# In-degree sums started in the encoder, and the general edge path moved to the program's end with a second copy of the network

## The chip, the core and the metric

The kernel runs on one core of a Trainium2 chip. A core has five engines, each with an instruction queue of its own that is worked off in order: PE (matrix multiplication; its weight loads are listed as PEld), DVE (vector), ACT (scalar), POOL (general purpose) and SP (which here only starts transfers). Sixteen DMA engines move data between the chip's memory and the core's on-chip memory. Engines wait for one another by semaphores. The metric is the device time of one execution in microseconds (us).

## The reference

The inputs are 1,250 nodes with 1,024 features and 20,000 edges (`src`, `dst`), sorted by `dst`. Two graph networks run one after the other, each inside a residual and a normalisation:

```python
h = layernorm(x, ln_in_g, ln_in_b)
h = relu(h @ W1 + b1) @ W2 + b2                      # encoder, 1024 -> 512 -> 256
for i in range(3):                                   # three layers
    agg = segment_sum(h[src], dst, num_segments=n)
    z = relu((h + agg) @ layer_Wa[i] + layer_ba[i]) @ layer_Wb[i] + layer_bb[i]
    h = h + relu(layernorm(z, layer_ng[i], layer_nb[i]))
delta = relu(h @ Wd1 + bd1) @ Wd2 + bd2              # decoder
x1 = norm(x + layernorm(x + delta, out_g, out_b))
...
deg = segment_sum(ones, dst); deg_inv = 1 / max(deg, 1)
h1  = relu(x1 @ W_self0 + (segment_sum(x1[src], dst) * deg_inv) @ W_neigh0 + b0)
out = h1 @ W_self1 + (segment_sum(h1[src], dst) * deg_inv) @ W_neigh1 + b1
out = norm(x1 + out)
```

The second network needs `deg`, the number of edges that end at each node: its in-degree.

## The kernel before, in words

**Nodes and numbers.** The nodes stand in ten tiles of 128 (the last one has 98 nodes and four spare rows). An fp32 matmul is made from three: each operand is split into a high and a low part (`split_w`, `relu_split`; ACT makes the high part, DVE or POOL the low one, L124, L125, L150 to L155), and `mm3` (L113 to L115) adds high x high, high x low and low x high. Names ending in h and l are these parts.

**Edges as a matrix.** All sums over edges are done with one dense matrix `A` of 1,254 x 1,254 edge counts (ten tiles of rows, AW columns). It is built during the encoder. The sorted edges stand in 157 tiles of 128, five to a group. For each group DVE builds one-hot matrices `R` (L333) and `Q` (L342, L344) from two arrays of codes (`rp`, `qp`) which `codes(0)` to `codes(2)` compute; PE multiplies them (`edge_tile`, L358) into `pa`, and ACT copies the block to `A` at a column that it reads from `anci` (`load_bases` L321, copy L364). POOL adds the one column that two groups share (L370). `ahead` and `some_edges` put these steps between the matmuls of the encoder.

**A fast and a general path.** This needs that each group's edges lie in a window of at most 51 nodes. The array `est` carries the edges, the windows' starts `anc` and their limits `atop`, `agap`. At the start DVE counts how many limits hold; the flag `fli` is 1 when some do not (L270, L272). `anci` is `anc` limited from above by `atop` (L264). `nc.values_load(fli)` (L389) loads the flag into a register on all five engines. `any_edges`, called before the encoder's second chunk of nodes, branches on it (L392): if it is set, `general_adjacency` builds the matrix from any edges, in the tile `acc` and scratch tiles (`spare` among them), and writes it to memory; a second branch (L578) loads it over `A`. With these inputs the flag is 0 and both branches are passed by.

**The encoder** goes over five chunks `PCH` of two tiles each. For a chunk: transposes of x (`transpose_x`, L445; ACT and DVE split the result into `h0h`, `h0l`, L448, L450), four column blocks `y_chunk(c, f)` of x @ W1 (with edge matmuls between them), and `h_rows(t)`, the product with W2, for each of the two tiles. `SLOTS` = 13 of these blocks carry edges. After the last of them the identity is added to `A` (L577), since h + agg is (A + 1) h.

**The layers.** `agg(i, c, t0, t1)` multiplies h by `A` for a range of columns (L649); ACT and DVE split the sum into `zh` and `zl` (L654, L655); `z1_chunk` and `z2_rows` are the layer's two products. Weights come through a ring of three buffers, `wraw`; `load_wab`, `load_Wd1` and `load_Wd2` (L615, L698, L707) fetch and split them. `load_xo` has SP write the output bias as rows of `xo_d` (L732) and POOL add x to them in memory by accumulating transfers (L736). `A` is written to `A_d` (L781) in layer 0, after the loads of the next layer's vectors. The second network reads it back.

**In-degrees.** `asum` is the sum of A's ten row tiles; `degrees()` (L601 to L606, in layer 1) sums it over the partitions, subtracts the identity and inverts. Before, tiles 0 to 5 are added ahead of layer 0 in five instructions of 1,254 columns (L744, L746), and tiles 6 to 9 in eight halves of 627 columns that the source has in layer 0 (L784).

**What sets the order.** In `manual_schedule` stretches (the start, the encoder's first chunk, and everything from the decoder's main loop on) the listed engines follow the source. Elsewhere a scheduler lays out each engine's queue by its own estimates; so an instruction can come earlier or later than its place in the source, but no instruction crosses a branch.

Of the kernel before, what the change touches and what calls it, by code (L numbers as in the profile page):

```python
# [21 lines left out]
P = 128  # L22
# [33 lines left out]
def gz(t):  # L56
    return P if t < NT - 1 else N - (NT - 1) * P + NG
# [3 lines left out]
    return P if t < NT - 1 else N - (NT - 1) * P  # L61


@with_exitstack
def tile_gnn(ctx, tc, x, es, vecs, W1, W2, b2, Wa, Wb, bb, ng, nb, Wd1, Wd2, bd2, og, ob,
             Ws0, Wn0, b0l, Ws1, Wn1, b1l, out):
    nc = tc.nc
    V, S, G, T = nc.vector, nc.scalar, nc.gpsimd, nc.tensor

# [95 lines left out]
    S1 = tc.alloc_tile_pool(name="S1", bufs=1, reuse_waits="tile")  # L165
    epsc0 = S1.tile([P, 1], F32, name="epsc0")

    est = S1.tile([P, 2 * NGR * GT + 3 * (NGR + 1) + 3 * GT], I32, name="est")
    ne, o = NGR * GT, 2 * NGR * GT
    esrc, edst = est[:, :ne], est[:, ne:o].rearrange("p (g j) -> p g j", j=GT)  # L170
    anc, atop, agap = (est[:, o + i * (NGR + 1):o + (i + 1) * (NGR + 1)] for i in range(3))
    o += 3 * (NGR + 1)
    woff, wwid, wend = (est[:, o + i * GT:o + (i + 1) * GT].unsqueeze(1).broadcast_to([P, NGR, GT])
                        for i in range(3))
    base, nbase = (anc[:, i:i + NGR].unsqueeze(2).broadcast_to([P, NGR, GT]) for i in range(2))
# [56 lines left out]
    with tc.high_priority(), tc.manual_schedule(engines=order):  # L232
        V.memset(epsc, EPS)
        S.activation(epsc0, epsc, AF.Sqrt)
        V.memset(ones, 1.0)
        iq = S1.tile([P, NT * WMAX], F16, name="iq")
        G.iota(iq, pattern=[[1, NT * WMAX]], base=1, channel_multiplier=0, allow_small_or_imprecise_dtypes=True)
        ir = S1.tile([P, P], BF16, name="ir")
        G.iota(ir, pattern=[[1, P]], base=0, channel_multiplier=0, allow_small_or_imprecise_dtypes=True)
        make_identity(nc, ident)  # L240
        dd, dn, blk = (S1.tile([P, NGR, GT], I32, name=nm_) for nm_ in ("dd", "dn", "blk"))
        va, vn = (S1.tile([P, NGR, GT], F32, name=nm_) for nm_ in ("va", "vn"))

        rp = S1.tile([P, NGR * GT, 2], BF16, name="rp")
        qp = S1.tile([P, NGR * GT, 2], F16, name="qp")
        q4 = S1.tile([P, NGR], F32, name="q4")
        vcnt = S1.tile([P, 1], F32, name="vcnt")
        anci = S1.tile([1, NGR + 1], I32, name="anci")
        ac, ad = (S1.tile([1, NGR + 1], F32, name=nm_) for nm_ in ("ac", "ad"))
        acnt = S1.tile([1, 2], F32, name="acnt")  # L250
        V.tensor_sub(dd, edst, base)
        V.tensor_sub(dn, edst, nbase)
        V.tensor_sub(dd, dd, woff)

        V.tensor_sub(ad[:, :NGR], anc[0:1, 1:], anc[0:1, :NGR])
        V.tensor_tensor(vn, dn, wend, ALU.is_lt)
        V.tensor_tensor(va, dd, wwid, ALU.is_lt)
        V.scalar_tensor_tensor(ac, anc[0:1], 0.0, atop[0:1], ALU.add, ALU.is_le, accum_out=acnt[:, 0:1])
        V.scalar_tensor_tensor(va, dd, 0.0, va, ALU.is_ge, ALU.mult)
        V.scalar_tensor_tensor(ad[:, :NGR], ad[:, :NGR], 0.0, agap[0:1, :NGR], ALU.add, ALU.is_le,  # L260
                               accum_out=acnt[:, 1:2])
        V.scalar_tensor_tensor(va, vn, 1.0, va, ALU.mult, ALU.mult, accum_out=vcnt)
        V.scalar_tensor_tensor(vcnt[0:1], acnt[:, 0:1], acnt[:, 1:2], vcnt[0:1], ALU.add, ALU.add)
        V.tensor_tensor(anci, anc[0:1], atop[0:1], ALU.min)  # L264
        warm_up(WA)
        st0 = bn(0)
        pc = pst("pc")
        T.matmul(pc[:1, 0:1], vcnt, ones[:, 0:1], start=True, stop=True)
        flf = S1.tile([1, 1], F32, name="flf")
        V.tensor_scalar(flf, pc[:1, 0:1], E + 2 * NGR + 0.5, None, ALU.is_lt)  # L270
        fli = S1.tile([1, 1], I32, name="fli")
        V.tensor_copy(fli, flf)  # L272
        warm_up(WB)

    def pairs(ap):
# [97 lines left out]

    def ahead(g):
        nonlocal n_oh
        while n_oh < min(NGR, g):
            one_hots(n_oh)
            n_oh += 1

    def some_edges(k):  # L380
        nonlocal n_ed
        for _ in range(k):
            ahead(n_ed // GT + LOOK + 1)
            if n_ed < ET:
                edge_tile(n_ed)
                n_ed += 1


    flag = nc.values_load(fli[0:1, 0:1], min_val=0, max_val=1)  # L389
    def any_edges():  # L390

        with tc.If(flag > 0):  # L392
            acc = Ap.tile([P, NT, AW], F32, name="acc", tag="A")
            V.memset(acc, 0.0)
            scratch = [B1.tile([P, 8 * (PW + 2)], F32, name=f"g{s}", tag=f"h0{s}0", bufs=1) for s in "hl"] + spare
            general_adjacency(tc, psp, acc[:, :, :N], (esrc, est[:, ne:2 * ne]), ident, ones, x, A_g, xg_d, scratch)
            res = Ap.tile([P, NT, AW], F32R, name="A", tag="A")
            nc.sync.dma_start(res.bitcast(F32)[:, :, :NN], A_g)
        return res


# [100 lines left out]
    with tc.manual_schedule(engines=order):  # L502
# [17 lines left out]
        warm_up(WC)  # L520
        transpose_x(0, (2,))
        split_W1(2)
        mv2 = bn_mv(bn(2), 2)
        split_W1(3)
        std2 = bn_std(mv2)
        split_W1(4)
        next(bn_norm(2, *std2))
        codes(0)
        for f in range(4):
            first[f] = pst("ps_y", "ps" if f < 2 else "pa")  # L530
        for k in range(8):
# [4 lines left out]
            if k == 0:  # L536
                transpose_x(0, (4,))
                split_W1(5)
                codes(1)
                mv3 = bn_mv(bn(3), 3)  # L540
            if k == 2:
                transpose_x(0, (6,))
# [1 line left out]
                std3 = bn_std(mv3)  # L544
                split_W1(7)
                next(bn_norm(3, *std3))
                codes(2)
            if k == 6:
                transpose_x(1, (0,))
        transpose_x(1, (2,))  # L550
        transpose_x(1, (4, 6))
        load_W2()
        V.tensor_copy(onesr, ones)
        ahead(2)
    for f in range(4):
        V.tensor_add(b1c[:, f:f + 1], first[f][:, PW:PW + 1], vec[:, C_B1 + f:C_B1 + f + 1])
    NC = len(PCH)
    SLOTS = 13
    for c in range(NC):
        if c == 1:  # L560
            A = any_edges()
        for f in range(4):
            slot = 4 * (c - 1) + f
            y_chunk(c, f, -(-(ET - n_ed) // (SLOTS - slot)) if 0 <= slot < SLOTS else 0)
# [5 lines left out]
            if f in (1, 2):  # L570
                if 2 * c + 3 + f < NT:
                    ln_x(2 * c + 3 + f)
            if slot == SLOTS - 1:

                for t in range(NT):
                    n = gz(t)
                    V.tensor_add(A[:n, t, t * P:t * P + n], A[:n, t, t * P:t * P + n].bitcast(F32), ident[:n, :n])  # L577
                with tc.If(flag > 0):  # L578
                    nc.sync.dma_start(A.bitcast(F32)[:, :, :NN], A_g)
    for t in PCH[NC - 1]:  # L580
        h_rows(t)
    B1.release()
# [158 lines left out]
    load_wab(0)  # L741
    begin_layer(0)
    load_xo()
    V.tensor_add(asum, A[:, 0, :NN].bitcast(F32), A[:, 1, :NN].bitcast(F32))  # L744
    for t in range(2, 6):
        V.tensor_add(asum[:gz(t)], asum[:gz(t)], A[:gz(t), t, :NN].bitcast(F32))  # L746
    for t0, t1 in ((0, 8), (8, NT)):
        agg(0, 0, t0, t1)
        agg(0, 1, t0, t1)
    for i in range(3):  # L750
# [28 lines left out]
        if i == 0:  # L779
            with tc.issue_after(loads["nb"].ins):  # L780
                nc.sync.dma_start(A_d, A.bitcast(F32)[:, :, :NN])  # L781
            for t in range(6, NT):
                for cs in (slice(0, NN // 2), slice(NN // 2, NN)):
                    V.tensor_add(asum[:gz(t), cs], asum[:gz(t), cs], A[:gz(t), t, cs].bitcast(F32))  # L784
            load_wab(2)
            for k in range(2):
                load_Wd2(k)
# [881 lines left out]
```

## Time and profile before

| | us |
|---|---|
| median of 3 timed runs | 923.88 (922.95 to 924.91) |
| the profiled execution | 923.78 |
| its span, first to last instruction | 921.9 |
| stage: encoder, to the last encoder rows | 0 to about 122 |
| stage: three layers | about 122 to 255 |
| stage: decoder | about 255 to 360 |
| stage: second network | about 360 to 919 |
| last ACT instruction (L1268) | 917.89, 0.81 long |
| issue of the last two output transfers (SP, L1269) | 918.34, 0.81 for both |

The page's second part shows the span in 40 equal slices of 23 us:

```profile
PE   7799998999899999999999999999999999999997
DVE  8799678595976775565677675547466786777785
...
PEclk9799999999999999999999999999999999999999
DMA  7310058953115649997442236537895722322214
```

Each digit is the busy share of a slice in tenths, PEclk the clock that PE was granted in tenths of full speed. The rows of instructions that follow below give start, duration and engine, and in brackets how long the engine had been idle and what ended that. "PEq", "DVEq" and so on are an engine's instruction sequencer, which handles branches and register loads.

### The profile page before, as it was taken

What the parts mean: (1) busy time and instruction counts of PE and PEld (TensorE: products, weight loads), DVE (VectorE), ACT (ScalarE), POOL (GpSimd) and SP (SyncE); (2) the same over time, 40 slices, a digit from 0 to 9 for tenths busy, and PEclk for the clock granted to TensorE, in tenths of its full rate; (3) what the DMA queues carried; (4) which work ended last, traced back from release to release, by engine and by line L of the source; (5) the groups of instructions that cost most, each with busy time, mean ns of one, the idle gap of its engine ahead of it and who ended that gap; (6) DMA issues with size and microseconds to landing.
All of it is one profiled execution on the core that took longest, in us unless ns stands there. A gap on an engine that the chain in (4) does not pass through costs nothing.

```text
span 921.9 us, 13248 instructions
## 1 busy us (share of the span) xinstructions
PE 894.7 (97%) x4777; PEld 788.2 (85%) x4783; DVE 645.0 (70%) x1311; ACT 394.2 (43%) x760; POOL 87.7 (10%) x122
## 2 busy tenths in 40 slices
PE   7799998999899999999999999999999999999997
PEld 6799998988887778999988888889999888888885
DVE  8799678595976775565677675547466786777785
ACT  4577523454566873211133354543111333333454
POOL 4022234344201000000000000000000000000000
PEclk9799999999999999999999999999999999999999
DMA  7310058953115649997442236537895722322214
GB/s 243 118 42 2 1 197 217 312 177 103 61 52 202 224 145 348 336 310 254 170 148 72 77 127 197 172 125 264 287 306 214 235 80 77 85 72 76 81 47 177
DMA packets 83666, 148.35 MB, mean 161 GB/s; under 512 B 8296, under 2 KB 31995, under 8 KB 83082
## 3 DMA queue, kind: packets, MB, share of 16 engines
q1 hardware_dynamic: 77206, 126.90, 41.4%
q0 software_dynamic: 2176, 10.27, 4.5%
q10 hardware_dynamic: 4212, 10.27, 3.0%
q8 instruction: 38, 0.62, 0.3%
q14 instruction: 34, 0.28, 0.1%
HBM read 103.35 MB, written 49.21 MB: 165 GB/s over the span
## 4 chain that ended last, share of the span: by engine, by line
PE 83%; DVE 6%; DMA 4%; ACT 1%; issue 1%; POOL 0%; ACTq 0%; DVEq 0%; POOLq 0%; SPq 0%
PE ps_A L1222 20%; PE ps_m L113 14%; PE ps_m L115 14%; PE ps_m L114 14%; DMA wraw<-in_Wd_dram 3%; PE ps_dd L113 2%; PE ps_dd L115 2%; PE ps_dd L114 2%; PE pa L358 2%; PE ps_y L113 2%; PE ps_y L114 1%; PE ps_y L115 1%; PE ps_z L649 1%; DVE asum L746 1%; PE pt L974 1%
## 5 line engine op out<-in xcount | busy, mean ns | idle before, releaser
L113 PE MATMUL ps_m<-w,th 128*128 128x512 f32 x520 | 204.1, 392 | 0.0
L115 PE MATMUL ps_m<-w,th 128*128 128x512 f32 x520 | 202.6, 390 | 0.0
L114 PE MATMUL ps_m<-w,th 128*128 128x512 f32 x520 | 202.3, 389 | 0.0
L1222 PE MATMUL ps_A<-A,qh 128*128 128x418 f32 (+1 forms) x480 | 170.5, 355 | 0.0
L1222 PE MATMUL ps_A<-A,ql 128*128 128x418 f32 (+1 forms) x480 | 169.9, 354 | 0.0
L115 PEld LDWEIGHTS ps_m<-w,th 128*128 128x128 f32 x520 | 97.6, 188 | 20.7
L113 PEld LDWEIGHTS ps_m<-w,th 128*128 128x128 f32 x520 | 97.6, 188 | 19.8
L114 PEld LDWEIGHTS ps_m<-w,th 128*128 128x128 f32 x520 | 97.7, 188 | 19.7
L125 DVE TENSOR_TENSOR w<-stage,w 128x512 fp32r<-128x512 f32 x65 | 44.7, 690 | 68.2 <-ACT w L124 67.9
L1222 PEld LDWEIGHTS ps_A<-A,ql 128*128 128x128 f32 (+1 forms) x480 | 90.8, 189 | 1.9
L124 ACT ACTIVATE w<-stage 128x512 fp32r<-128x512 f32 x65 | 40.7, 629 | 118.8 <-PE ps_m L115 76.7
L1222 PEld LDWEIGHTS ps_A<-A,qh 128*128 128x128 f32 (+1 forms) x480 | 90.3, 188 | 1.2
L1227 DVE TENSOR_TENSOR MT<-ps_A,dgb 128x418 f32<-128x418 f32 x48 | 25.5, 586 | 64.6 <-PE ps_A L1222 64.6
L1183 ACT ACTIVATE qh<-qraw 128x1280 fp32r<-128x1280 f32 (+3 forms) x28 | 21.5, 809 | 105.1 <-PE ps_A L1222 102.8
L113 PE MATMUL ps_y<-h0h,w1h 128*128 128x256 f32 (+2 forms) x160 | 52.9, 331 | 0.0
L125 DVE TENSOR_TENSOR w<-wraw,w 128x512 fp32r<-128x512 f32 x39 | 26.9, 689 | 32.5 <-ACT w L124 30.7
L114 PE MATMUL ps_y<-h0l,w1h 128*128 128x256 f32 (+2 forms) x160 | 46.3, 289 | 2.9 <-DVE h0l L450 2.9
L1311 DVE TENSOR_TENSOR c<-ps_m,c 128x512 f32<-128x512 f32 (+1 forms) x65 | 40.9, 682 | 8.8 <-PE ps_m L115 8.7
L115 PE MATMUL ps_y<-h0h,w1l 128*128 128x256 f32 (+2 forms) x160 | 45.9, 287 | 0.0
L1052 ACT ACTIVATE th<-XT 128x640 fp32r<-128x640 f32 x48 | 34.2, 724 | 20.5 <-DVE MT L1227 20.5
L124 ACT ACTIVATE w<-wraw 128x512 fp32r<-128x512 f32 x39 | 24.5, 628 | 41.6 <-PE ps_m L115 21.3
L1053 DVE TENSOR_TENSOR th<-XT,th 128x640 fp32r<-128x640 f32 x48 | 39.5, 822 | 0.0
(307 smaller groups left out, 1842.4 us busy)
## 6 DMA issues: line engine op xcount, KB each, us to landing
A<-A_d SPq DMA_DIRECT2D x20, 627.0 KB
w_d<-stage SPq DMA_DIRECT2D x43, 256.0 KB
stage<-w_d SPq DMA_DIRECT2D x43, 256.0 KB
stage<-in_l_W_neigh_dram SPq DMA_DIRECT2D x42, 256.0 KB
stage<-in_l_W_self_dram SPq DMA_DIRECT2D x28, 256.0 KB
A_d<-A SPq DMA_DIRECT2D x1, 6270.0 KB
wraw<-in_l_W_neigh_dram SPq DMA_DIRECT2D x22, 256.0 KB
w_d<-wraw SPq DMA_DIRECT2D x21, 256.0 KB
```

The costliest lines, as they stand in the source:

```text
L113: T.matmul(ps, a_hi, b_hi, start=start, stop=False, skip_group_check=go_on)
L114: T.matmul(ps, a_hi, b_lo, start=False, stop=False, skip_group_check=go_on)
L115: T.matmul(ps, a_lo, b_hi, start=False, stop=stop, skip_group_check=go_on)
L124: S.activation(hi, raw, AF.Copy)
L125: return eng.tensor_sub(lo, raw, hi.bitcast(F32))
L358: T.matmul(pa[g][:, :, lo:hi], R[:, j], Q[j], start=j == 0, stop=end, skip_group_check=True)
L1052: S.activation(hi, src, AF.Copy)
L1053: V.tensor_sub(lo, src, hi.bitcast(F32))
L1183: S.activation(q[0][:, t0:t1], raw[:, t0:t1], AF.Copy)
L1222: T.matmul(pss[j][c][:, :w], qs[j][s][:n, t], A_of(t)[:n, c0:c0 + w], start=start and s == 0, stop=stop and s == 1)
L1227: V.tensor_mul(MT[:, f, c0:c0 + w], pss[j][c][:, :w], dgb[:, c0:c0 + w])
L1311: V.tensor_add(c, ps[:n], c if last or M in (6, 7) else c11[:n, t])
```

## The change

- `tile_gnn` becomes a small frame around the function `gnn`. It calls `gnn` once with `general=False`, then loads the flag and, if it is set, runs `gnn` a second time with `general=True`. The second call is a full copy of the network's instructions with `general_adjacency` in it; each engine jumps over it when the flag is 0. The two branches inside the network (L392, L578) and the flag load before them are gone. PE's queue grows from 5,081 rows to 9,622, DVE's from 1,294 to 2,299, ACT's from 828 to 1,459 and SP's from 345 to 649; what is added, and the general path, stand behind the new branch.
- The first pass now runs to its end even when the flag is set, so `anci` must be safe then: where any window or gap check fails, evenly spaced starts (`even`, 33 further columns of `est`) are taken. One operation on 33 elements becomes four on 1 to 33 elements, and they stand later, ahead of the third tile's statistics.
- `codes(0)`, `codes(1)` and `codes(2)` each move one place later in the encoder's first chunk.
- The in-degree sums of tiles 0 to 4 (`EARLY` = 4: eight halves) are made right after the identity has been added, in the last edge slot of the encoder. They go to `spare[0]`, a buffer that so far only the general path used. Tiles 5 to 9 (ten halves) follow ahead of layer 0; nothing of it is left in layer 0.

As laid out, the changed kernel's queues also differ in a few neighbours. On PE four transposes of x stand six warm-up matmuls earlier at the start. In the encoder's second chunk DVE has the bn_stats and the low part of one y block behind the transposes' low parts, where they had been ahead of them, and `qp` and `q4` (codes(2)) after the cast of `onesr`.

```diff
+def tile_gnn(tc, *args):
+    with tc.tile_pool(name="keep", bufs=1) as keep:
+        fli = keep.tile([1, 1], I32, name="fli")
+        gnn(tc, fli, False, *args)
+        flag = tc.nc.values_load(fli, min_val=0, max_val=1)
+        with tc.If(flag > 0):
+            gnn(tc, None, True, *args)
...
-        V.tensor_tensor(anci, anc[0:1], atop[0:1], ALU.min)
         warm_up(WA)
...
-        fli = S1.tile([1, 1], I32, name="fli")
-        V.tensor_copy(fli, flf)
+        if not general:
+            V.tensor_copy(fli, flf)
...
-    flag = nc.values_load(fli[0:1, 0:1], min_val=0, max_val=1)
     def any_edges():
-        with tc.If(flag > 0):
-            acc = Ap.tile([P, NT, AW], F32, name="acc", tag="A")
...
+        acc = Ap.tile([P, NT, AW], F32, name="acc", tag="A")
...
         transpose_x(0, (2,))
         split_W1(2)
+        V.tensor_tensor(acnt[:, 0:1], acnt[:, 0:1], acnt[:, 1:2], ALU.add)
+        V.tensor_scalar(acnt[:, 0:1], acnt[:, 0:1], 2 * NGR + 0.5, None, ALU.is_gt)
+        V.tensor_sub(ac, anc[0:1], even[0:1])
+        V.scalar_tensor_tensor(anci, ac, acnt[:, 0:1], even[0:1], ALU.mult, ALU.add)
         mv2 = bn_mv(bn(2), 2)
...
-        codes(0)
...
-                codes(1)
+                codes(0)
                 mv3 = bn_mv(bn(3), 3)
...
-                codes(2)
+                codes(1)
...
         V.tensor_copy(onesr, ones)
+        codes(2)
         ahead(2)
...
+    HALVES = (slice(0, NN // 2), slice(NN // 2, NN))
+    EARLY = 4
...
         if c == 1:
-            A = any_edges()
+            A = any_edges() if general else Ap.tile([P, NT, AW], F32R, name="A", tag="A")
...
-                with tc.If(flag > 0):
-                    nc.sync.dma_start(A.bitcast(F32)[:, :, :NN], A_g)
+            if slot == SLOTS - 1:
+                sums = [spare[0][:, cs] for cs in HALVES]
+                for t in range(1, EARLY + 1):
+                    for half, cs in zip(sums, HALVES):
+                        V.tensor_add(half, A[:, 0, cs].bitcast(F32) if t == 1 else half, A[:, t, cs].bitcast(F32))
...
-    V.tensor_add(asum, A[:, 0, :NN].bitcast(F32), A[:, 1, :NN].bitcast(F32))
-    for t in range(2, 6):
-        V.tensor_add(asum[:gz(t)], asum[:gz(t)], A[:gz(t), t, :NN].bitcast(F32))
+    for t in range(EARLY + 1, NT):
+        for half, cs in zip(sums, HALVES):
+            V.tensor_add(asum[:gz(t), cs], (half if t == EARLY + 1 else asum[:, cs])[:gz(t)],
+                         A[:gz(t), t, cs].bitcast(F32))
...
-            for t in range(6, NT):
-                for cs in (slice(0, NN // 2), slice(NN // 2, NN)):
-                    V.tensor_add(asum[:gz(t), cs], asum[:gz(t), cs], A[:gz(t), t, cs].bitcast(F32))
```

## The prediction

> **What bounds the kernel now.** I read the page's engine totals first, then PE's waits, then the stretches in which PE is not full, then the rows in them. The profiled run took 923.78 us: a span of 921.9 us and 1.9 us around it; the median of the three timed runs is 923.88, so a sum made against the profiled run holds for the median to 0.1 us. The totals, and PE's waits (us in total, times, longest):
>
> ```profile
> PE 894.7 (97%) x4777; PEld 788.2 (85%) x4783; DVE 645.0 (70%) x1311; ACT 394.2 (43%) x760; POOL 87.7 (10%) x122
> PE ps_h L113 <- PEq L392: 4.0, 1, 4.0
> PE ps_z L114 <- DVE zl L655: 3.2, 1, 3.2
> PE ps_y L114 <- DVE h0l L450: 2.9, 2, 2.0
> ```
>
> PE is the bound: only 27 us of the span are not PE's. Three of its waits (4.0, 3.2, 2.0) lie where the change works, with a second loss behind each: PE's granted clock. The stretches:
>
> ```profile
> core 0: us, PE busy (x) PEld busy (x) DVE busy (x) ACT busy (x) POOL busy (x), PEclk, DMA share, GB/s
> 30.00:40.00 10.00, 5.36 (x37) 4.47 (x35) 8.67 (x28) 7.04 (x18) 0.00 (x0) 0.97 0.45 162
> 40.00:45.00 5.00, 4.70 (x23) 4.33 (x23) 1.67 (x6) 1.63 (x4) 0.21 (x1) 0.50 0.02 5
> ...
> 60.00:70.00 10.00, 10.00 (x87) 9.43 (x85) 9.79 (x33) 6.91 (x20) 1.52 (x4) 1.00 0.32 94
> ...
> 130.00:140.00 10.00, 8.66 (x40) 6.99 (x38) 9.93 (x11) 2.31 (x5) 0.89 (x1) 1.00 1.02 406
> 140.00:150.00 10.00, 8.17 (x38) 7.62 (x39) 6.46 (x12) 3.70 (x6) 5.00 (x6) 0.83 0.68 189
> ```
>
> The reader is to see: a hole at 30 to 40, then a stretch at clock 0.50; from 60 on PE and DVE are both full (so the encoder is a race of two engines); at 130 to 150 DVE is full, PE is not, and the clock falls to 0.83.
>
> **Step 1, the mid-program branch goes.** The rows of line 392, durations in ns:
>
> ```profile
> L392 DVEq COMPARE_BRANCH  x1: 76/76/76, 34.3 to 34.3; - x1
> L392 SPq COMPARE_BRANCH  x1: 45/45/45, 35.7 to 35.7; - x1
> L392 PEldq COMPARE_BRANCH  x1: 3858/3858/3858, 36.3 to 36.3; - x1
> ```
>
> PE stood still for 3.86 us in the branch, DVE for 1.33 (its next work starts at 37.32). It would be wrong to book 4.0 us: while PE stood, DVE made the one-hots (R, Q) and the yl that PE needs next. So I walk DVE's queue in the order in which the changed kernel is built. Up to the cast of onesr (ends 35.3) it has 1.2 us less in front (a bn_stats 0.68, a yl 0.4 and nmm now come later) and starts 0.3 earlier (step 2): 33.8. Then qp 0.5, yl 0.35, q4 0.2, two groups of R and Q at 1.1 each (37.80 to 38.91 in the trace), nmm 0.1, yl 0.35, bn_stats 0.7, yh 0.2, aggregate 0.1, R 0.4, yl 0.35: 39.3. Group 2's Q with two reciprocals and the 0.8 us normalisation L303: 41.2. R and Q of group 3: 42.3. PE, which waits for each of these, then transposes (0.4 us) and begins the next y chunk at about 42.9; before, it began at 46.4 with group 3's five edge matmuls (0.6 us) still to do. That is 4.1 us, DVE-bound. From there both engines keep their order. The branch of line 578 cost PE's queue 0.22 us with PE full: nothing.
>
> Here a rule speaks against the change. The Trainium skill (TensorE: Matmul & The Clock Gate, Part 1) says that PE's clock halves after a window of about 3.4 us without enough activity. By the rows alone, the hole goes and the 0.50 of 40 to 45 with it (23 matmuls, up to 2 us). By the rule nothing of that returns, because PE, waiting for DVE, is only about half busy from 33 to 43, and the y chunk begins at half speed: 24 matmuls at 0.216 us instead of 0.12 (both spacings stand at 22 to 28 us) would cost 2.3. I take 0.8 off: **3.3 us** gained, ends 1.0 and 5.5.
>
> **Step 2, codes and anci.** Before, PE waited 2.00 us at 21.03 because codes(0) (1.33 and 1.44 us, 17.78 to 20.51) stood on DVE ahead of h0l. Now h0l comes first, but four operations on 1 to 33 elements (rows of 0.17, some 0.6 us together) have been put ahead of it and codes(0) ahead of the next bn_stats. What is late next: the h0l that the seventh k needs. It follows after codes(0), 2.77, and the statistics, 1.5; I get about 23.5 for its start, 23.96 before. PE runs from 18.9 through two k's (24 x 0.12) and waits again at 21.8 for 2.1 us. The DVE chain up to xs (26.80) loses codes(1), 1.35, and gains 0.6; PE's warm-ups, now behind its first transposes, cost 0.25. Net 0.3, already used above. The 33 more columns of est (16 KB) cost nothing against the 1.15 us wait of DVE for them.
>
> **Step 3, in-degree sums.** Before, DVE ran five adds of 1254 columns and, ahead of zl, the eight halves that the code has in layer 0 (DVE's timeline; the last row is PE's):
>
> ```profile
> 122.62 1.46 DVE L744 TENSOR_TENSOR asum<-A 128x1254 f32<-128x1254 f32 x1
> 124.12 9.59 DVE L746 TENSOR_TENSOR asum<-asum,A 128x1254 f32<-128x1254 f32 x3
> ...
> 135.45 5.87 DVE L784 TENSOR_TENSOR asum<-asum,A 128x627 f32<-128x627 f32 x8
> 141.23 2.21 DVE L655 TENSOR_TENSOR zl<-ps_z,zh 128x384 fp32r<-128x384 f32 x4
> 141.83 0.69 PE L114 MATMUL ps_z<-zl,wabh 128*128 128x384 f32 x1 [3.17 <-DVE zl L655]
> ```
>
> Now ten halves stand there: 10 x 0.73 = 7.3 us. If POOL's splits stretch one as they did (one add took 5.6 instead of 1.45, +4.2), they end 11.5 us after 122.6, at 134.1, and zl's input is complete only at about 136. So PE's 3.17 us go, and the ten matmuls behind them run at 0.19 instead of 0.32: 1.3. Together **4.5 us**. The other eight halves, 5.9 us, go between L577 (ends 112.5) and yh (114.17). They end at 118.4; then yh, yl, yl by 119.4. The last yh waits for ACT until 119.54 anyway and PE asks for these operands at 119 to 120. DVE's own idle (1.65 + 2.46 + 1.80 us) is the cover; POOL is idle from 113.4 to 121.7, so nothing stretches them. Cost 0; without that cover up to 4.2 (rival C).
>
> **Step 4, what is late next: DMA.** From 131 to 197 the DMA engines are nearly full with xo_d's write (issued 128.8), POOL's accumulates (to about 175) and A_d (from 172.2), and Wd's loads queue behind (timelines of ACT and PE):
>
> ```profile
> 200.85 0.63 ACT L124 ACTIVATE wd<-wraw 128x512 fp32r<-128x512 f32 x1 [2.16 <-DMA wraw<-in_Wd_dram]
> 202.64 0.43 PE L113 MATMUL ps_z<-zh,wabh 128*128 128x358 f32 x1 [1.22 <-ACT zh L654]
> ```
>
> PE's wait at 202.64 is already that chain. xo_d moves 3.3 us forward with the encoder, A_d 7.8. From its new issue at 164.4 there is 1.6 MB of accumulate left (7.7 us at 213 GB/s), A_d's 6.27 and 1.3 of weights: 9.2 MB at the 351 GB/s of 172 to 196 is 26.2 us, to 190.6; compute would want 188.3. So **2.3 us** are given back on ACT, with ends 0 (accumulates and A_d share well) and 4.5 (all of step 3).
>
> **Step 5, the new end.** Each engine now loads the flag (0.47 to 0.54 us, rows of L389) and jumps over the second network. SP's flag load stands early, its jump behind the last output DMA, issued until 919.15; that DMA's landing is awaited at 921.1. DVE and ACT reach it at about 918.4. The jump is not in the trace at this distance. Nearest row for SP: 0.5 us from compare to next event at L392, hidden: 0. The rule: the skill (Runtime: NRT & Kernel Launch, Instruction fetch mechanics) says an engine holds two pages of 256 instructions (PE more) and that a taken branch beyond them must fetch the page by DMA first. The skipped copy is over 400 rows on SP and thousands on PE, so SP misses too; at PE's price, 3.86, it arrives at 923.0, 1.9 late. I take **1.3**, nearer the miss, ends 0 and 2.5.
>
> **Sum:** 923.78 - 3.3 - 4.5 + 2.3 + 1.3 = **919.6 us**.
>
> **Rivals.** *A, DMA takes all of step 3* (for: ACT already waits 6.0 us for Wd; against: the accumulates leave a third of the bandwidth): 923.78 - 3.3 + 1.3 = 921.8. *B, everything goes through*: PE's clock stays up in the encoder (3.3 + 0.8 + 1.2 of step 2's slow stretch), 4.5, lag 1.0, end hidden: 915.0. *C, the early sums don't do what they are for*: POOL stretches one of the eight as it did L746, yh comes 4.2 us late to the last rows of the encoder: 923.8, no change; against it stands POOL's idle row. *D, slower: the end jump.* The place is behind the last output DMA, where nothing covers it. Should the five engines' fetches queue behind each other, 5 x 3.9 = 19 us from 919.2, 17 beyond today's end: 923.78 - 5.5 + 17 = 935. It decides from a miss of 7.4 us on the last engine; against it, at L392 all five were through within 4.0 us.
>
> **How the numbers follow.** Forecast 0.50 (own range 917.5 to 921.7), A 0.18, B 0.15, C 0.08, D 0.09. A difference under 0.2% (1.85 us) is not told from none here. Faster: nearly all of the forecast, half of A, all of B, 0.72; slower: D and a little of C, 0.10; same: the rest, 0.18. The range leaves out D, the low half of B and the bad end of C: 915.2 to 924.0.
>
> **What would show it.** No PE wait at L392 and y chunk 1,1 starting about 4 us earlier (step 1); the 2 us wait at h0l moved to k = 6, not gone (2); no PE wait for zl, clock 1.00 there (3); ACT's waits for Wd longer than 2.16 us and PE's wait for zh longer than 1.22 (4); a span that ends later than the landing of the last output (5). I am wrong if the wait before layer 0 turns up again behind yh, or if the tail grows by more than 2.5 us.

## The result, and the profile after

The changed kernel takes 927.5 us at the median of nine runs (925.0 to 928.7), the kernel before 923.2; the ratio is 1.004, with a 95% interval of 1.003 to 1.0051. It is slower, by 4.3 us at the medians and 3.7 by the ratio, where 4.2 us less had been forecast, and it lies above the range. The profiled execution took 928.25 us.

From the page of the changed kernel, the span and the totals:

```profile
span 926.5 us, 13243 instructions
...
PE 896.4 (97%) x4783; PEld 787.7 (85%) x4783; DVE 643.4 (69%) x1319; ACT 393.7 (42%) x760; POOL 99.0 (11%) x122
```

PE's work is the same (894.7 before). POOL has nothing new to compute in the first network, yet it is busy for 11.3 us more: that is the first hint. PE's waits (us in total, times, longest):

```profile
PE ps_z L123 <- ACT zh L672: 3.1, 1, 3.1
PE ps_z L697 <- DMA bbc<-wraw: 3.0, 1, 3.0
...
PE ps_y L124 <- DVE h0l L457: 0.9, 2, 0.5
```

The waits at the branch (4.0), for zl (3.2) and most of those for h0l (2.9) are gone, as planned. In their place stand a wait for `bbc`, the bias row of layer 0, which did not exist before, and one for zh that was 1.2. The stretches of time that were shown of before:

```profile
core 0: us, PE busy (x) PEld busy (x) DVE busy (x) ACT busy (x) POOL busy (x), PEclk, DMA share, GB/s
30.00:40.00 10.00, 8.89 (x66) 7.47 (x65) 9.92 (x33) 8.14 (x20) 0.00 (x0) 1.00 0.48 159
40.00:50.00 10.00, 8.74 (x56) 7.65 (x56) 8.87 (x31) 7.29 (x21) 3.37 (x5) 0.83 0.00 1
130.00:140.00 10.00, 10.00 (x50) 8.74 (x49) 6.22 (x10) 4.76 (x9) 2.33 (x2) 1.00 0.92 367
140.00:150.00 10.00, 7.04 (x38) 6.46 (x37) 5.13 (x15) 2.49 (x5) 3.47 (x6) 0.83 0.65 210
200.00:210.00 10.00, 6.76 (x30) 6.18 (x30) 7.94 (x18) 4.75 (x11) 8.71 (x8) 0.83 0.27 80
```

The hole at 30 to 40 has closed. At 130 to 140 PE is now full at full clock (8.66 before), but the hole has only moved: it stands at 140 to 150, with the same clock of 0.83, and a second one at 200 to 210, where PE was at clock 1.00 before. (A mean clock of 0.83 over 10 us is 1.7 us of PE's clock lost.)

To place the difference I cut the program at three marks on PE's timeline: the first aggregation of layer 0 (L667), the last matmul of z2 (L697) and the last matmul of all.

| us | before | after | difference |
|---|---|---|---|
| start to first aggregation (encoder) | 121.95 | 120.16 | -1.8 |
| to the last z2 (three layers) | 134.5 | 138.2 | +3.7 |
| to the last matmul | 658.5 | 658.4 | -0.1 |
| to the end of the span (tail) | 7.0 | 9.7 | +2.7 |

All marks are starts of matmuls. 923.78 - 1.8 + 3.7 - 0.1 + 2.7 is 928.3, the profiled execution. So two places are to be explained: the layers, which should have gained 2.2 us, and the tail.

**The layers.** DVE's timeline around the eight early halves and the ten late ones (start, duration, idle time before), and then POOL's over the same times:

```profile
110.28 1.52 DVE L597 TENSOR_TENSOR spareh<-A 128x627 f32<-128x627 f32 x2
111.72 4.41 DVE L597 TENSOR_TENSOR spareh<-spareh,A 128x627 f32<-128x627 f32 x6
...
120.84 1.53 DVE L764 TENSOR_TENSOR asum<-spareh,A 128x627 f32<-128x627 f32 x2
122.28 4.41 DVE L764 TENSOR_TENSOR asum<-asum,A 128x627 f32<-128x627 f32 x6
131.60 1.21 DVE L135 TENSOR_TENSOR wraw<-wraw,bbc 1x256 f32<-1x256 f32 x1 [4.91 <-ACT bbc L134]
132.75 1.51 DVE L764 TENSOR_TENSOR asum<-asum,A 102x627 f32<-102x627 f32 x2
```

```profile
110.50 6.42 POOL L500 TENSOR_TENSOR hil<-hf,hih 128x256 fp32r<-128x256 f32 x1 [0.26 <-ACT hih L499]
119.90 0.74 POOL L500 TENSOR_TENSOR hil<-hf,hih 128x256 fp32r<-128x256 f32 x1 [2.98 <-ACT hih L499]
120.83 7.03 POOL L135 TENSOR_TENSOR wabl<-wraw,wabh 128x512 fp32r<-128x512 f32 x1 [0.18 <-ACT wabh L134]
```

The same POOL subtraction takes 0.74 us at 119.90 and 6.42 at 110.50, while DVE runs eight halves (110.28 to 116.13); the split of `wab` takes 7.03 while DVE runs eight more, and ends 1.2 us after the last of them, about one undisturbed duration (1.3). By these ends POOL did not work in that time: it waited for DVE. The same split took 2.62 us before:

```profile
122.61 2.62 POOL L125 TENSOR_TENSOR wabl<-wraw,wabh 128x512 fp32r<-128x512 f32 x1 [0.19 <-ACT wabh L124]
```

It frees a buffer of the weight ring, for which SP's queue waits:

```profile
127.88 0.38 SPq L633 DMA_DIRECT2D wraw<-in_layer_Wb_dram  x1
...
130.15 0.38 SPq L750 DMA_DIRECT2D xo_d<-o  x1
...
132.84 0.64 SPq L649 DMA_DIRECT2D bbc<-wraw  x1
```

Before, the Wb load stood at 125.26 and xo_d's write at 128.77, with an encoder that ended later. So xo_d starts 1.4 us later in place of 1.8 earlier, `bbc`'s row, queued behind its 5 MB, lands at 146.4, PE waits 3.0 us for it, and the stream of accumulates, A_d and Wd ends later too (ACT gets its first Wd at 197.75, 196.11 before), which is the wait for zh.

**The tail.** The rows of the branch line at the end (durations in ns, then start times in us):

```profile
L70 PEldq COMPARE_BRANCH  x1: 3522/3522/3522, 913.6 to 913.6; - x1
...
L70 DVEq COMPARE_BRANCH  x1: 76/76/76, 920.2 to 920.2; - x1
L70 ACTq COMPARE_BRANCH  x1: 50/50/50, 920.3 to 920.3; - x1
L70 SPq COMPARE_BRANCH  x1: 53/53/53, 921.1 to 921.1; - x1
L70 ACTq EVENT_SEMAPHORE  x1: 17/17/17, 923.2 to 923.2; - x1
L70 DVEq EVENT_SEMAPHORE  x1: 21/21/21, 923.3 to 923.3; - x1
```

DVE compares at 920.2 and does its next thing 3.2 us later; ACT needs 2.9 us, SP 3.1 (921.1 to 924.2). The jumps run side by side, so their times do not add up. PE's is hidden, as it has finished. SP, the last, holds up the end in two ways. It comes back at 924.2, 3.6 us after its last output was issued (920.64); before, that output had landed 2.2 us after its issue (918.76 to 921.0), so 1.4 us are added. And SP's checks of its semaphores now stand behind the jump:

```profile
L70 SPq EVENT_SEMAPHORE  x8: 17/17/17, 924.2 to 924.8; - x8
L1682 SPq EVENT_SEMAPHORE  x14: 17/28/28, 924.8 to 926.4; - x14
```

The eight of the first row and twelve of the second take until 925.5, 1.3 us; before, there were only the twelve, made while the output was landing (L1665, 919.2 to 921.0). 1.4 + 1.3 is the tail's 2.7. In this trace the last parts of the output also landed later than before, 3.2 us after the issue; whether the jumps caused that is not shown.

### The profile page after: what moved, and what is told of

The parts are those of the page before. It is cut to its first block, busy times and chain, and to the rows that moved or that the text cites. A ratio compares the mean times of both kernels' runs of the same rounds, so it can differ in the third digit from the quotient of the medians.

```text
span 926.5 us, 13243 instructions
## 1 busy us (share of the span) xinstructions
PE 896.4 (97%) x4783; PEld 787.7 (85%) x4783; DVE 643.4 (69%) x1319; ACT 393.7 (42%) x760; POOL 99.0 (11%) x122
## 4 chain that ended last, share of the span: by engine, by line
PE 70%; DVE 10%; DMA 8%; ACT 5%; issue 3%; POOL 2%; POOLq 0%; ACTq 0%; SPq 0%; DVEq 0%
PE ps_A L1238 20%; PE ps_m L123 13%; PE ps_m L124 13%; PE ps_m L125 13%; DMA wraw<-in_Wd_dram 3%; DMA bbc<-wraw 2%; DMA x_d<-vt 1%; ACT vt L156 1%; ACT junk L882 1%; PE pa L367 1%; DVE vt L899 1%; PE ps_y L123 1%; PE ps_z L667 1%; ACT ut L882 1%; PE pt L1259 1%
```

## Experiments

All ratios are to the kernel before, timed on the same chip alongside, with 95% intervals. "Layers" is the stretch from the first aggregation to the last z2 (134.5 before, 138.2 after), "split" the first wab split on POOL, "xo_d" the issue of its write. These columns are of one profile each, and hold some chance of the clock (below).

| run | ratio | first agg. | layers | split | xo_d |
|---|---|---|---|---|---|
| e1 no end branch | 1.0001 (0.9991 to 1.0012) | 120.1 | 137.2 | 7.0 | 130.1 |
| e2 old sums, end branch | 0.9987 (0.9974 to 1.0001) | 117.8 | 132.8 | 2.6 | 124.6 |
| e3 before + new sums | 1.0032 (1.0021 to 1.0044) | 123.1 | 136.8 | 7.0 | 133.1 |
| e4 before, no branches | 0.9973 (0.9964 to 0.9981) | 116.7 | 133.1 | 2.6 | 123.5 |
| e5 meant as e9, was the changed kernel | 1.0047 (1.003 to 1.0064) | 119.8 | 137.9 | 7.0 | 129.8 |
| e6 full adds | 0.9999 (0.9988 to 1.001) | 120.0 | 133.5 | 2.6 | 126.9 |
| e7 bbc on ACT's queue | 1.0038 (1.0023 to 1.0054) | 118.0 | 137.8 | 7.0 | 128.0 |
| e8 branch hint | 1.0049 (1.003 to 1.0069) | 118.5 | 139.5 | 7.0 | 128.5 |
| e9 chained halves | 0.9968 (0.9956 to 0.998) | 119.8 | 132.1 | 2.0 | 125.3 |
| e16 full adds in two sums | 1.0049 (1.0032 to 1.0066) | 118.7 | 138.3 | 8.1 | 129.8 |
| e17 e9 + A_d late | 0.9972 (0.9964 to 0.998) | 120.1 | 130.3 | 2.0 | 125.6 |

### The change taken apart: e1 to e4

e1 is the changed kernel without the last two lines of `tile_gnn`; e2 has the old sums back; e3 is the kernel before with the new sums, e4 the kernel before without L392 and L578 (and without the flag's load, L389).

```diff
 # e1
         gnn(tc, fli, False, *args)
-        flag = tc.nc.values_load(fli, min_val=0, max_val=1)
-        with tc.If(flag > 0):
-            gnn(tc, None, True, *args)
 # e4
-            A = any_edges()
+            A = Ap.tile([P, NT, AW], F32R, name="A", tag="A")
...
-                with tc.If(flag > 0):
-                    nc.sync.dma_start(A.bitcast(F32)[:, :, :NN], A_g)
```

> The changed kernel without the branch at the end and without the second copy of the network (the general path is left out). Theory T: the tail behind the last matmul, 9.7 us, goes back to 7.0, and nothing else moves: 927.5 - 2.7 = 924.8, still slower than the kernel before (ratio 1.0017), because the in-degree sums lose 3.7 in the layers. Rival 1 (the jump lies beside the landing of the last output and the closing barrier): at most 1 us, 926.5. Rival 2 (all of the loss is the second copy): 920.5 to 922.

> The changed kernel with the in-degree sums in their old place (five full adds ahead of layer 0, eight halves in layer 0); the end branch stays. Theory T: the half adds that run back to back on VectorE keep GpSimd's two splits of wab waiting, which frees the weight buffer late and delays bbc, xo_d and Wd; with the old adds that goes, and the wait for zl comes back: the encoder's gain of 1.8 stays, the tail's loss of 2.7 stays, so 923.2 - 1.8 + 2.7 = 924.1, and the wab split is back near 2.6 us from 7.0. Rival DMA (it is the earlier encoder that makes the transfers collide, and the sums help by the wait for zl): the wait of 3.2 us for zl comes on top, 929 to 930.5.

> The kernel before with the new in-degree sums alone (eight halves in the encoder, ten ahead of layer 0), both branches of the old program kept. Theory T: the sums lose 3.7: 926.9; PE waits for bbc about 3 us, the wait for zl is gone. The prediction's steps 3 and 4 as they stood: 923.2 - 2.2 = 921.0.

> The kernel before without its two branches in the middle (the general path is left out), sums in the old place. Theory T: the encoder ends 1.8 earlier and all of it arrives: 921.4. The prediction's step 1 as it stood: 923.2 - 3.3 = 919.9. Rival DMA (transfers behind the encoder take the gain back): 922.5 to 923.5.

Measured medians: 923.5, 922.35, 926.4 and 920.4 us. e1 is 1.3 below theory T; e4 lies nearer to the prediction's step 1 than to T. The end branch costs 3.6 us by e1 (0.0039 of 923), 1.3 by the pair e2 and e4, around the 2.7 that the two traces show. The new sums cost 3.0 us by e3, 4.9 by e2: theory T was within 0.5 us for e3 and 1.8 too high for e2. The mid-program branches are worth 2.5 us (e4). So the branch's move is close to even, and the sums are the loss. In e2 the wait for zl is back (3.3 us), with the layers at 132.8: the rival that the earlier encoder makes the transfers collide falls.

e2 and e4 have the old sums and the wait for zl (3.3 and 3.2 us), but their layers take 132.8 and 133.1 us and not 134.5. The difference is PE's clock behind that wait:

```profile
137.00:147.00 10.00, 6.83 (x26) 5.93 (x25) 7.76 (x13) 3.05 (x7) 2.00 (x4) 0.83 0.71 258
137.00:147.00 10.00, 9.30 (x58) 8.78 (x59) 7.80 (x21) 4.10 (x8) 5.21 (x6) 1.00 0.82 196
```

The first row is of the kernel before, the second of e2; the columns are those of the stretches above, with the clock third from the end. The same wait drew a slow stretch, worth 1.7 us, in one run and none in the other. Differences of that size between two entries of the layers column show nothing by themselves.

### What keeps POOL out: e5, e6, e9, e16

The Trainium skill has a rule for this (SBUF — State Buffer, "SBUF: two separate sides"): it says that a DVE operation with two operands in SBUF and a GpSimd operation that reads SBUF exclude each other, and that whichever starts first has the port pair for the whole instruction. By that rule POOL would wait for one add, 0.8 us. It waited for six to eight. Two differences to the old adds were open: the new ones are short, and they alternate between two halves, so that none reads what its neighbour wrote.

e6 takes full adds (`HALVES = (slice(0, NN),)`); e9 chains the halves: all of one, then all of the other, with an ordering edge between the two.

```diff
 # e9 (in the encoder likewise)
-    for t in range(EARLY + 1, NT):
-        for half, cs in zip(sums, HALVES):
-            V.tensor_add(asum[:gz(t), cs], ...
+    for half, cs in zip(sums, HALVES):
+        for t in range(EARLY + 1, NT):
+            with (tc.issue_after(last.ins) if last and t == EARLY + 1 else contextlib.nullcontext()):
+                last = V.tensor_add(asum[:gz(t), cs], ...
```

> The changed kernel with its half adds in another order: all of one half first, then all of the other, so that each add reads what the add before it wrote. Same number, same operands. Theory T1 (what keeps GpSimd out is not the adds but that they overlap: in the trace halves that do not depend on each other start 0.735 us apart and take 0.80, so VectorE never lets go of the port they share, while the old chained full adds left 0.04 us between two): GpSimd gets in behind the first add, wab's first split is back to 2 to 3 us from 7.0, PE's wait for bbc (3.0) goes and the wait for zl does not come back: 919 to 922. Rival T2 (any unbroken row of adds keeps GpSimd out): wab's split stays at 7, 927.5.

> The changed kernel with full adds of 1254 columns in place of halves (four in the encoder, five ahead of layer 0). T1: as with the chained halves, 919 to 922, a GpSimd split waits for one add of 1.45 us. T2 (any unbroken row of adds): 927.5. T3 (it is the length of an add, short ones keep GpSimd out): 919 to 922 here, but 927.5 with the chained halves.

> The changed kernel with the half adds truly chained: an added ordering edge holds the second half back until the first half is through, so every add but one waits for the add before it (in e5 the scheduler had put the two halves back in turn, so that it was the changed kernel once more). T1 (what keeps GpSimd out is that neighbouring adds overlap): GpSimd's first wab split is back to some 2 us, xo_d's write is issued about 3 us earlier, and the time is that of the full adds, 923.5. T3 (short adds keep it out): split 7 us, 927.5.

e5 had the loops turned as in e9 but no ordering edge; the scheduler put the halves back in turn, so it is one more run of the changed kernel (928.2 us). e6 came to 923.5 us, 1.5 above what T1 had given it and well below T2's 927.5, and e9 to 921.6, better than expected. e9's DVE and POOL timelines:

```profile
120.48 0.81 DVE L770 TENSOR_TENSOR asum<-spareh,A 128x627 f32<-128x627 f32 x1
121.32 8.50 DVE L770 TENSOR_TENSOR asum<-asum,A 128x627 f32<-128x627 f32 x4
```

```profile
120.47 1.97 POOL L136 TENSOR_TENSOR wabl<-wraw,wabh 128x512 fp32r<-128x512 f32 x1 [0.18 <-ACT wabh L135]
122.39 1.31 POOL L501 TENSOR_TENSOR hil<-hf,hih 102x256 fp32r<-102x256 f32 x1
123.67 3.79 POOL L136 TENSOR_TENSOR wabl<-wraw,wabh 128x512 fp32r<-128x512 f32 x3
```

The first add ends at 121.29 and the second is listed from 121.32: between chained adds there is a gap of some 0.03 us. POOL comes in there, does five operations in a row until 127.46, and now DVE stands (four adds in 8.50 us in place of 3.3). POOL's rows overlap as well: the first ends at 122.44, the second starts at 122.39. The adds end no later for it (134.1; 134.3 in the changed kernel), and the transfers start 4.8 us earlier. That leaves the length of an add as a rival, which e16 excludes: full adds into two running sums in turn, with ordering edges, one add more.

> The changed kernel with full adds of 1254 columns that do not read each other's result (two running sums in turn, one add more in all; the early part is two adds). T1 (neighbouring adds that overlap keep GpSimd out, whatever their length): the first wab split waits for all five, 7 us or more, and PE waits for bbc; 927 or more. T3 (only short adds do): split 2.6 us as with the chained full adds, 923.5.

Measured 927.9 us. e16's DVE timeline, and POOL's:

```profile
119.37 1.46 DVE L761 TENSOR_TENSOR asum<-spareh,A 128x1254 f32<-128x1254 f32 x1
120.75 1.46 DVE L765 TENSOR_TENSOR sparel<-sparel,A 128x1254 f32<-128x1254 f32 x1
...
124.87 1.46 DVE L765 TENSOR_TENSOR asum<-asum,A 128x1254 f32<-128x1254 f32 x1
```

```profile
119.36 8.13 POOL L135 TENSOR_TENSOR wabl<-wraw,wabh 128x512 fp32r<-128x512 f32 x1 [0.18 <-ACT wabh L134]
```

The full adds now start 1.37 to 1.38 us apart and are 1.46 long: they overlap by 0.08, and POOL stands through all five (8.13 us). Length does not matter. What is shown: neighbours that overlap keep POOL out until the row ends, neighbours that depend on each other let it in.

In time e9 is 6 us below the changed kernel. Against e2, which has the old sums, its ratio is lower by 0.0019 (1.8 us), and the two intervals overlap: chaining removes the loss, but a gain over the old sums is not shown by these two.

### Is it the bias row, or the stream? e7, e10 to e15, e17, e18

e7 writes `bbc`'s row from ACT's queue, past xo_d.

> The changed kernel with the one row of bbc for layer 0 written by ScalarE's queue in place of SyncE's, where it stands behind the 5 MB write xo_d<-o. The row lands before it is needed: if PE's wait for bbc (3.0 us, with the slower clock behind it some 4) is the main part of the loss in the layers, 923.5. Rival DMA (the loss is that all transfers behind xo_d run later, and the wait for bbc only lies ahead of the same wait for Wd): the wait moves to zh at 203, and 926.5 to 927.5 stays.

928.1 us: nothing gained. The wait for bbc is gone, but the one for zh is 6.2 us in place of 3.1. The rival is right here: PE's waits in layers 0 and 1 are slices of one delay, that of the stream that begins with xo_d. So I took parts of the stream away: xo_d into the encoder, in five pieces (e10; with full adds and a branch hint e11; in the kernel before e12), or behind Wd's last load (e13; with e9's chain e14; in the kernel before e15).

```diff
 # e10
+        if c == 1 and not general:
+            nc.sync.dma_start(spare[1][:, :D], bcast(ob, D))
...
+            if 0 <= slot < 5 and not general:
+                write_xo(spare[1][:, :D], 2 * slot)
+            if 7 <= slot < 12 and not general:
+                add_x(2 * (slot - 7))
 # e13
-    load_xo()
...
+            last = load_Wd2(3)
             load_bdo()
+            with tc.issue_after(last.ins):
+                load_xo()
```

> The changed kernel with xo_d (its 5 MB write and the accumulates of x) written during the encoder, in five pieces, out of a spare buffer, in place of behind bbc's load; nothing else is moved by hand. Theory T4 (layers 0 and 1 are set by one stream of transfers: in all runs so far layer 2's first z1 starts 72 to 74 us after xo_d's write is issued, 202.6 - 128.8 before, 203.7 - 130.2 after, 199.8 - 126.9 with full adds; so what a change gains ahead of that write's issue counts and what it gains behind it does not): with 10 MB out of that stretch PE's waits for bbc (3.0) and zh (3.2) and the slow clock behind each (about 1 each) go: 919.5 to 921.5. Rival (GpSimd's late splits hold PE up directly): 925 to 927.

> Full adds, xo_d in the encoder and the branch hint one row before the last (in e8 it was early: VectorE's jump took 0.6 us in place of 3.1, those of ScalarE and SyncE still 3.1). T4: full adds give 923.5; PE's wait for zh (4.1) and the slow clock behind it (1) go, the jump's 2.7 too: 916. If the hint works on VectorE alone: 918.5. Rival as in e10: 921 to 923.

> The kernel before with xo_d written during the encoder, as in e10, all else as before. T4: here PE waits for zh for only 1.2 us and for zl for 3.2; the first goes, the second stays: 921.5 to 922.5. If it gains much more (919 or less), the stream of transfers had been holding up the old kernel too, and the gain of e10 says little about the change.

> The changed kernel with xo_d's write and accumulates behind the last Wd load (about 215 us) in place of behind bbc's load (130): the same 10 MB taken out of the stretch of layers 0 and 1, without the encoder's x loads in its way, which cost e10 to e12 some 11 us. T4 (layers 0 and 1 are bound by that stream of transfers): from the first aggregation to the last z2, 138.2 us in the changed kernel and 127.8 in e10, falls to 128 to 131, and the time is 918 to 921. Rival: the ten halves and GpSimd's splits bind layer 0 by themselves, 926 or more. A wait for the first decoded rows, if xo_d lands too late, would take some of it back.

> As e13, with the chained half adds of e9. T4 together with T1: bbc's load no longer stands behind xo_d, so the chained order is worth little here, 0 to 2 us below e13: 917 to 920. If T1 and T4 add up in full (e9's 6 us and e13's gain), 914.

> The kernel before with xo_d late as in e13: the control. There the wait for zl (3.2 us, sums in layer 0) is still behind the adds: 134.5 us from first aggregation to last z2 as in e12 (134.9), so 922 to 924. If it is 919 or less, the gain of e13 is not one of the early sums.

| run | median | ratio | first agg. | layers |
|---|---|---|---|---|
| e10 | 931.2 | 1.008 (1.0068 to 1.0093) | 133.3 | 127.8 |
| e11 | 931.6 | 1.0082 (1.0067 to 1.0098) | 133.6 | 128.9 |
| e12 (before) | 930.9 | 1.0071 (1.0055 to 1.0087) | 130.9 | 134.9 |
| e13 | 933.2 | 1.0101 (1.0084 to 1.0118) | 118.9 | 128.3 |
| e14 | 933.9 | 1.0104 (1.0088 to 1.0119) | 121.7 | 129.3 |
| e15 (before) | 939.0 | 1.0161 (1.0145 to 1.0177) | 122.0 | 134.7 |

As times, all six expectations failed. Early, in e10, POOL's queue stood 8.5 us at the fifth accumulate (66.34) until the write had landed, its column adds for A behind it, and the encoder lost 13 us. PE also waited longer for h0h, the split of x (4.8 us, 0.4 in the changed kernel); how the 13 us divide is not shown. Late, the decoder's first row waited for xo_d, in e13 among PE's waits:

```profile
PE ps_d L123 <- DVE ut L875: 13.0, 1, 13.0
```

But the layers column is what the theory said, in both places: without xo_d the changed kernel's layers take 128 to 129 us, with chained or overlapping adds alike, and the old sums 134.7 to 134.9, their wait for zl (3.2) still there. So without xo_d the early sums are worth 5 to 7 us in the layers (up to 1.7 of it the slow clock that e12 and e15 show behind their wait for zl), and the stream is what takes that away. e17 and e18 tried to have both, on top of e9: A_d behind layer 1's Wd loads, or xo_d there.

```diff
 # e17
-            with tc.issue_after(loads["nb"].ins):
-                nc.sync.dma_start(A_d, A.bitcast(F32)[:, :, :NN])
             load_wab(2)
...
-            load_Wd2(2)
+            with tc.issue_after(load_Wd2(2).ins):
+                nc.sync.dma_start(A_d, A.bitcast(F32)[:, :, :NN])
```

> The chained half adds of e9, and A's copy to DRAM (A_d, 6.3 MB) behind the six Wd loads of layer 1 in place of ahead of them. T4: the Wd loads no longer stand behind A_d, ScalarE's waits for them and with these PE's wait for zh (2.6 in e9) and the slow clock behind it go, and A_d runs in layer 2, where the transfer engines are idle and A is free only at about 247: first aggregation to last z2 goes from 132.1 to 128 to 129, the time from 921.6 to 917.5 to 918.5. If A_d only moves the wait to bbc of layer 2, which stands behind it in SyncE's queue: 920 to 922.

> The chained half adds of e9, and xo_d's write and accumulates right behind the Wd loads of layer 1 (about 197), some 18 us earlier than in e13 and e14, where the decoder's first rows waited 13 us for it. If those 13 us go: 918 to 920 with 128 to 129 from first aggregation to last z2. The bbc row of layer 2 and Wd's last four loads now stand behind the write (14 us): if layer 2 waits for bbc, 922 to 928.

e17: 920.5 us, layers 130.3, 1.8 below e9 where 3 to 4 had been expected: ScalarE now meets the Wd loads at 172 to 180, and PE waits 1.6 us for zh there. e18: 931.9 us (1.0097, 1.0082 to 1.0113), since `bd`'s load stands behind xo_d, ScalarE waits 11.3 us at it and PE 10.6 for zh of layer 2. The best kernels that keep the general path are e9 and e17, both below the kernel before by some 0.3% and not told apart by their intervals.

### The jump at the end: e8

A branch prefetch hint on DVE, ACT and SP, some rows before the end:

```diff
+        if not general and tt == 7:
+            for e, i_ in ((mybir.EngineType.DVE, rs_), (mybir.EngineType.Activation, sd_), (mybir.EngineType.SP, ins)):
+                with tc.issue_after(i_.ins):
+                    tc.mark_branch_hint_location("end", "LikelyTaken", engines=[e])
```

> The changed kernel with a hint (a branch prefetch hint that the jump at the end is likely taken) on VectorE, ScalarE and SyncE, set among the last rows of the output; nothing else is moved. If the 3 us from compare to next event are the fetch of the target and the hint starts that fetch early, they shrink to below 0.5 us on these engines and the tail by about 2.7: 924.5. If the time is something else (a drain, the barrier) or the hint does nothing here: 927.5.

928.2 us, no gain. The branch line's rows in e8:

```profile
L70 SPq EVENT_SEMAPHORE  x8: 17/17/17, 923.8 to 924.3; - x8
...
L70 DVEq COMPARE_BRANCH  x1: 89/89/89, 919.6 to 919.6; - x1
L70 ACTq COMPARE_BRANCH  x1: 68/68/68, 919.8 to 919.8; - x1
L70 DVEq EVENT_SEMAPHORE  x1: 21/21/21, 920.2 to 920.2; - x1
L70 SPq COMPARE_BRANCH  x1: 73/73/73, 920.6 to 920.6; - x1
L70 ACTq EVENT_SEMAPHORE  x1: 17/17/17, 923.0 to 923.0; - x1
```

On DVE the jump takes 0.6 us in place of 3.2. That the hint shortens it speaks for the fetch of the target as what the 3 us are; on ACT and SP, which still take 3.2, it is not shown. SP sets the end. In e11 the hint stood nearer the end, with the same outcome. Why it helps on one engine alone stays open.

## Why the prediction missed, by its own steps

**Step 1 (branch, 3.3 us): right in size, the clock a matter of chance.** In the two first traces the encoder ends 1.8 us earlier, but this mark moves by up to 4 us between profiles of one encoder. Over the 13 profiles of the changed encoder's own form (after, e1, e2, e5 to e9, e13, e14, e16 to e18) the first aggregation starts at 119.6 on average, over three of the old one (before, e3, e15) at 122.3: 2.8 us. e4, with the branch alone gone, gains 2.5 in time. The walk along DVE was right too: from the end of the cast of onesr to y chunk 1,1 it has 9.1 us (33.8 to 42.9), and the trace has 9.1 (35.71 to 44.79). But it starts 1.9 us late (step 2), so the chunk began 1.6 us earlier than before and not 4. The clock rule that the prediction quotes came true in part: in the profiled run the chunk's first nine matmuls stand 0.21 us apart, with a mean clock of 0.83 at 40 to 50. e1, e14, e17 and e18 have such a stretch too, the other eight of the 13 have none, and their first aggregation starts at 118.9 on average, against 120.5.

**Step 2 (codes, 0.3): mis-sized, a loss.** The wait for h0l did not move to the seventh k as 2.1 us; it is 0.9 in two pieces. But the chain up to xs, which was to end 0.3 us earlier, ends at 28.19, 1.4 later than before (28.3 on average over the 13, 26.8 over the three). Two terms were too small. The four operations on anci were put at 0.6 us. Here are two of them in the changed kernel, and POOL's rows beside them:

```profile
15.79 1.07 DVE L531 TENSOR_TENSOR acnt<-acnt 1x1 f32<-1x1 f32 x1
...
16.97 1.18 DVE L533 TENSOR_TENSOR ac<-est 1x33 f32<-1x33 int32 x1
```

```profile
15.56 1.30 POOL L135 TENSOR_TENSOR w1l<-wraw,w1h 128x512 fp32r<-128x512 f32 x1 [1.27 <-ACT w1h L134]
16.81 1.29 POOL L135 TENSOR_TENSOR w1l<-w1r,w1h 128x512 fp32r<-128x512 f32 x1
```

Each ends within 0.1 us of the POOL subtraction beside it: on 1 and 33 elements DVE waited for POOL. All four take 2.6 us (15.79 to 18.35), in every one of these profiles. And the warm-ups behind the first transposes were put at 0.25: the first y matmul starts at 13.84, 11.91 before, with a mean clock of 0.86 at 10 to 20 us (1.00 before) slowing the warm-ups.

**Step 3 (sums): the step that failed.** The wait for zl went, and the early eight cost the encoder nothing. Wrong was what it said of POOL: "If POOL's splits stretch one as they did", and for the early halves "POOL is idle from 113.4 to 121.7, so nothing stretches them". Both look only at what POOL does to DVE. What DVE does to POOL was not priced at all. The old adds were chained and let POOL in after one; the new ones overlap and do not, so the wab split took 7.0 us in place of 2.6 and xo_d started at 130.2 in place of 125.3. e9, which changes the order of the adds and nothing else, gives the layers 132.1 in place of 138.2, 6.1 us, and the whole 921.6 in place of 927.5. That the ten halves ended at 134.26, with 134.1 forecast, is luck: they began 1.8 us earlier than in the forecast's frame, no add was stretched, and the time went into 4.9 us in which DVE stood for the late bbc row.

**Step 4 (transfers, 2.3 us back): about right once POOL is let in.** Steps 3 and 4 together said -2.2 for the layers; e9 shows 132.1 - 134.5 = -2.4, but only -0.7 against e2, which had no slow clock behind its wait for zl. The two terms, 4.5 gained and 2.3 given back, are nearer 5.4 (e15 against e14, both without xo_d) and 2.8 (e9 against e14). The 351 GB/s that it read at 172 to 196 is 339 in the trace, 0.9 us more for its 9.2 MB. What it assumed, that xo_d moves forward with the encoder and A_d to 164.4, holds in e9 (xo_d 125.3, 3.5 us earlier than before; A_d 165.8) and not in the changed kernel (130.2 and 171.4). Rival A had the same mechanism and also took xo_d's early issue for granted.

**Step 5 (end, 1.3): the jump right, a term left out.** The tail grew by 2.7 us, more than the 2.5 that the prediction named as a sign of being wrong. Each of three engines misses, for 2.9 to 3.2 us, side by side, and SP is back 1.4 us after the output would have landed at the pace of before. So the 1.3 was met, though as a middle between "hidden" and PE's price of 3.86, not as SP's own price of 3.1. Left out were SP's checks behind the jump, 1.3 us, which could no longer run beside the landing. Rival D's queue of fetches did not occur.

Together: 919.6 + 0.5 (steps 1 and 2) + 6.1 (step 3) - 0.2 (step 4) + 1.4 (step 5) = 927.4. That this closes so well is in part chance, as the terms come from single profiles.

## What to carry to other kernels

When vector work is moved, look at what GpSimd has in the same stretch, in both directions: whether it stretches the moved instructions, however small they are, and whether they let it in. Partial sums that alternate between accumulators look better for the vector engine and can shut GpSimd out for their whole length; one chained accumulator lets it in at every step. And before a wait is booked as a gain, follow the transfers: if a stream of them ends just behind the stage, only what starts that stream earlier counts.

## What the runs showed of the hardware that I had not expected

- The exclusion between DVE and GpSimd is not per instruction. With DVE instructions that overlap (0.735 us apart and 0.80 long, or 1.38 apart and 1.46 long), a GpSimd subtraction of 0.7 to 1.3 us took 6.4, 7.0 and 8.1 us and ended 0.8 to 1.2 us after the row; with a gap of 0.03 us between two it took 2.0. The rule quoted above, one instruction at a time, fits the chained adds and not these. It works the other way too: GpSimd's five operations in a row held the DVE adds up for 5.2 us (8.50 us for four adds of 0.81), and a DVE operation on one element took 1.07 us beside a subtraction.
- A jump to a far target took 2.6 to 3.4 us on DVE, ACT and SP in all profiles with the branch at the end and no hint, 3.3 to 3.9 on PE. A prefetch hint brought DVE's to 0.6 and left ACT's and SP's at 3.2. Work that used to run beside a wait and now stands behind such a jump (SP's 20 checks, 1.3 us) comes on top.
